# A block of gated cross-attention and FFN on one core: products of the last group reordered by tokens, one sum of M moved

## The chip, the cores and the metric

The kernel runs on one core of a Trainium2 chip. The metric is the device time of one execution in microseconds (us). Engines are named as in the profile: PE is TensorE (PEld its weight loads), DVE is VectorE, ACT is ScalarE, POOL is GpSimd, SP is SyncE, which here only issues transfers.

## The reference, cut to what matters

```python
# x (4, 2048, 512), context (4, 77, 384), 16 heads of 64, all float32
def _layernorm(x): return (x - mean(x)) / sqrt(var(x) + 1e-5)      # over the last axis, 512 wide

def attention(x, context):                    # Wq (512,1024), Wk, Wv (384,1024), Wo (1024,512)
    q, k, v = heads(x @ Wq), heads(context @ Wk), heads(context @ Wv)
    out = softmax(q k^T / 8) v
    return merge(out) @ Wo + bo

def ffn(x):                                   # W (8,512,512), b (8,512): one of eight is picked
    idx = argmax(log_softmax(logits) - log(-log(u)))
    return x @ W[idx] + b[idx]

x = x + tanh(g_xattn) * attention(_layernorm(x), context)
x = x + tanh(g_ffn)   * ffn(_layernorm(x))
```

## The kernel before

The 8192 tokens are worked on in 16 groups of 512; four groups share one context. For each of the four contexts the weights are folded ahead: M stands for Wq with the keys (scores are x times M), vo for the values with Wo. So a group has three large products: the scores (`ps_s`, from the columns of x and M), the attention output (`ps_a`, from the softmax weights `pT` and `vo`), and the FFN (`ps_f`, from the residual stream `xc` and the picked weight `wf`).

Each large product is made by `Seven`, the scheme of seven products of half-size blocks in place of eight. The columns are split in a 2 x 2 grid: B11, B12, B21, B22, where the first digit is the half of the contraction and the second the half of the group's tokens (256 each). T1 to T4 are sums and differences of these (`Columns.sum`: T1 = B12 - B11, T2 = B22 - T1, T3 = B22 - B12, T4 = B21 - T2), made on POOL. On the weights' side blocks 4 to 6 are such sums too, and block 3 becomes one (`weight_sum`: block 5 = 0 - 3, then 3 = 3 + 2, 4 = 3 - 0, 6 = 1 - 4). `ORDER` lists the seven products: block of the weight, column block, PSUM bank r, and whether the bank starts anew:

```python
ORDER = ((0, "B11", 0, True), (3, "T1", 1, True), (4, "T2", 0, False), (1, "B21", 2, True),
         (5, "T3", 0, False), (6, "B22", 1, False), (2, "T4", 0, False))
```

Products that share r accumulate in one bank, and `post` takes intermediate states out: `keep` copies a bank to SBUF on ACT (L469 without, L473 with the bias), or DVE adds a bank to what was kept (L486). The result's quarters are named by two digits: half of the features, half of the tokens.

Around it, in a steady group i, with j = i - 1: the exps of group i run on ACT beside the attention products of group j; DVE transposes between rows and columns (`x_columns` L412, `to_rows` L417, `s_rows` L515, `p_columns` L552); POOL makes the T sums (L437), the scaling of the softmax by its sums (`head_scale` L543) and the residual additions (`residual` L558). `residual_last` (L565) is on DVE, straight from PSUM. `y_rows` turns the residual stream back into rows, `f_rows` the FFN's output. The second layer norm is applied behind the FFN: `Norms` takes statistics of y (`stats` L370), sums them over partitions with two small products on TensorE (`mean`, `var`, L375), and raises to -1/2 on POOL (`rstd` L409). The scaled FFN output (`f_scale` L586, on ACT) is added to y (`f_add` L590) and stored (`store` L594, four transfers for a group, by quarter of the features).

Every engine's queue is in the order in which the code issues (a schedule by hand): an instruction that waits holds all that stands behind it on its engine. In the groups i = 3, 7 and 11 (`swap_m`), M of the next context is loaded (`load_m`) and its four `weight_sum` are made: numbers 0, 2 and 3 on POOL, number 1 on DVE at the end of the attention products (L877).

The last group has no successor whose scores could fill TensorE. Its attention products, its FFN products, and the scaling and storing that remain stand in the tail of the function, from `j, f = NGRP - 1, NGRP - 2` on. There `by_feature` (h = half of the features in a quarter row, v = half of the group's rows) splits the last scaling in four, which are spread over POOL, ACT and DVE by `scaled`. The last transfers are issued as `store(j, 0, 8, ...)` and `store(j, 8, 8, ...)`, each in four transfers of 128 KB over the queues of SP and ACT.

Of the kernel before, what the change touches and what calls it, by code (L numbers as in the profile page):

```python
# [10 lines left out]
AF = mybir.ActivationFunctionType  # L11
ALU = mybir.AluOpType
AX = mybir.AxisListType

P = 128
# [4 lines left out]
def flamingo_block_kernel(  # L20
# [337 lines left out]
    class Norms:  # L358


        def __init__(self, i):
            self.y = 2 <= i
            self.x = i < NGRP
            self.n = NG * (self.y + self.x)
            self.x0 = NG * self.y
            self.s6 = small.tile([P, self.n, 6], F32, tag="s6", name="s6")

# [29 lines left out]
        def rstd(self):  # L397
            self.rs = small.tile([P, self.n], F32, tag="rs", name="rs")
            nc.vector.tensor_scalar(self.rs, self.ps[:, 1], EPS, None, ALU.add)  # L399
            if self.x:  # L400
                r = self.rs[:, ds(self.x0, NG)]
                nc.gpsimd.tensor_tensor(r, r, neghalf, ALU.pow)  # L402
                self.up = small.tile([P, NG], F32, tag="up", name="up")
                self.down = small.tile([P, NG], F32, tag="down", name="down")
                nc.gpsimd.tensor_scalar(self.down, r, -SCALE, None, ALU.mult)
                nc.gpsimd.tensor_scalar(self.up, r, SCALE, None, ALU.mult)
            if self.y:
                r = self.rs[:, :NG]
                nc.gpsimd.tensor_tensor(r, r, neghalf, ALU.pow)  # L409

    def to_columns(dst, src, q):
        nc.vector.transpose(dst[:, q, :].rearrange("p (g c) -> p g c", c=32), src[:, :, ts(q, 32)])  # L412
# [32 lines left out]
    class Seven:  # L445
# [1 line left out]
        ORDER = ((0, "B11", 0, True), (3, "T1", 1, True), (4, "T2", 0, False), (1, "B21", 2, True),  # L447
                 (5, "T3", 0, False), (6, "B22", 1, False), (2, "T4", 0, False))

        def __init__(self, name, w, cols, pairs, snap, bias=None):  # L450
            self.name, self.w, self.cols, self.pairs, self.bias = name, w, cols, pairs, bias
            self.n = len(pairs)
            self.low, self.high = snap
            self.ps = [None] * 3

        def product(self, s):
            blk, cname, r, first = self.ORDER[s]
            if first:
                self.ps[r] = bank(self.name)[:, : self.n * T2].rearrange("p (n t) -> p n t", n=self.n)
            h = self.cols.h  # L460
            for n, pair in enumerate(self.pairs):
                for c in range(h):
                    nc.tensor.matmul(self.ps[r][:, n, :], self.w(blk, c, pair), self.cols(cname, c),  # L463
                                     start=(first and n == 0 and c == 0), stop=(c == h - 1),
                                     skip_group_check=True)
# [11 lines left out]
            return (self.low, self.high)[int(which[0]) - 1][:, :, int(which[1]) - 1, :]  # L477

        def post(self, s):
            if s in (0, 1, 2, 6):  # L480
                which, r = (("11", 0), ("22", 1), ("12", 0), None, None, None, ("21", 0))[s]
                self.keep(self.quarter(which), r, int(which[0]) - 1)
            else:
                which, r = {3: ("11", 2), 4: ("22", 0), 5: ("12", 1)}[s]
                c = self.quarter(which)
                nc.vector.tensor_tensor(c, c, self.ps[r], ALU.add)  # L486

# [276 lines left out]
    for i in range(1, NGRP):  # L764
# [67 lines left out]
        for s in range(7):  # L832
            at.product(s)
            if s == 0:
                pT[j].sum("T2")
                if 0 <= f:
                    f_scale(f, n.rs, 10, 6)
                    f_add(f, 0, NG, nc.gpsimd)
                    store(f)
                head_max(i, 0)  # L840
                head_max(i, 1)
            if s == 1:
                head_max(i, 2)
                head_max(i, 3)
            if 1 <= s:
                e = (0, 10, 20, 32, 44, 56, 64)
                exps(i, e[s - 1], e[s])
            if s == 0 and i == 1:
                weight_sum(vo, 3)
                pT[j].sum("T3")  # L850
            if s == 1 and i == 1:
                scale_wf(wfr)
            if s == 2:
                pT[j].sum("T4")
                if swap_m:
                    weight_sum(m, 0)
                if not last:
                    x_columns(nx)
                    norms[nx].stats(xg[nx], norms[nx].x0, 0, 8)
                head_sum(i, 0)  # L860
                head_scale(i, 0)
            if s == 3:
                if not last:
                    norms[nx].stats(xg[nx], norms[nx].x0, 8, 8)
                    if nx + 1 < NGRP:
                        load(nx + 1)
            if s == 4:
                residual(j, at, "11")
                head_sum(i, 1)
                head_scale(i, 1)  # L870
            if s == 5:
                head_sum(i, 2)
                head_scale(i, 2)
                residual(j, at, "22")
            if s == 6:
                if swap_m:
                    weight_sum(m, 1, nc.vector)  # L877
                residual(j, at, "12")
                residual_last(j, at)
                head_sum(i, 3)  # L880
            else:
                at.post(s)
# [11 lines left out]
        for s in range(6):  # L894
            ff.product(s)
            if s < 2:
                y_rows(j, 2 * s)
            if not last:
                if s == 1:
                    xc[nx].sum("T1")  # L900
                if s == 2:
                    xc[nx].sum("T2")
                if s == 4:
                    if swap_m:
                        weight_sum(m, 2)
                    xc[nx].sum("T3")
                    if swap_m:
                        weight_sum(m, 3)
# [6 lines left out]

    j, f = NGRP - 1, NGRP - 2
    n = norms[NGRP] = Norms(NGRP)
    pT[j].sum("T1")
    at = Seven("ps_a", w_attend, pT[j], (0, 1), SNAP, bo_c)
    for s in range(7):  # L920
        at.product(s)
        if s == 0:
# [13 lines left out]
            pT[j].sum("T4")  # L936
        if s == 3:
            n.rstd()
        if s == 4:
            f_scale(f, n.rs, 0, NG)  # L940
            residual(j, at, "11")
        if s == 5:
            residual(j, at, "22")
            f_add(f, 0, NG, nc.vector)
            store(f)
        if s == 6:
            residual(j, at, "12")
            residual_last(j, at)
            for q in (0, 2):
                y_rows(j, q, 1)  # L950
        elif 0 < s:
            at.post(s)
    yc[j] = Columns(xc[j].all, **{f"T{k + 1}": tq[:, k] for k in range(4)})
    for t in ("T1", "T2", "T3", "T4"):
        yc[j].sum(t)
    n = Norms(NGRP + 1)
    ff = Seven("ps_f", w_ffn, yc[j], (0, 1), SNAP)

    def by_feature(t, h, v):

        return t[:, ts(v, NG // 2), ts(h, D // NA // 2)]

    def scaled(h, v, engine):

        d, y = by_feature(ts_[j], h, v), by_feature(ys[j], h, v)
        r = n.rs[:, ts(v, NG // 2)]
        if engine is nc.vector:
            for g in range(NG // 2):
                nc.vector.scalar_tensor_tensor(y[:, g, :], d[:, g, :], r[:, g : g + 1], y[:, g, :],
                                               ALU.mult, ALU.add)  # L970
            return
        if engine is nc.scalar:
            for g in range(NG // 2):
                nc.scalar.activation(d[:, g, :], d[:, g, :], AF.Copy, scale=r[:, g : g + 1])
            return
        engine.tensor_tensor(d, d, r.unsqueeze(2).to_broadcast(list(d.shape)), ALU.mult)
        engine.tensor_tensor(y, y, d, ALU.add)

    for s in range(6):
        ff.product(s)  # L980
        if s == 0:
            n.stats(ys[j], 0, 8, 8)
            y_rows(j, 0, 0)
            y_rows(j, 2, 0)
            n.stats(ys[j], 0, 0, 8)
            for v in (1, 0):
                y = ys[j][:, ts(v, NG // 2)]
                nc.gpsimd.tensor_tensor(y, y, bf_r.unsqueeze(1).to_broadcast([P, NG // 2, P]), ALU.add)
        if s == 2:
            n.mean()  # L990
            n.spread()
        if s == 3:
            n.var()
            n.rstd()
        ff.post(s)
        if s == 3:
            f_rows(j, ff, 0, 0)
            scaled(0, 0, nc.gpsimd)
        if s == 4:
            f_rows(j, ff, 1, 1)  # L1000
            scaled(1, 1, nc.scalar)
        if s == 5:
            f_rows(j, ff, 0, 1)
            scaled(0, 1, nc.scalar)
    ff.product(6)
    for k in range(2):
        to_rows(ts_[j], ff.ps[0][:, k, :], 2 + k, 0)
    scaled(1, 0, nc.vector)
    store(j, 0, 8, (nc.sync, nc.scalar))
    for h in (1, 0):  # L1010
        y = by_feature(ys[j], h, 1)
        nc.vector.tensor_tensor(y, y, by_feature(ts_[j], h, 1), ALU.add)
    store(j, 8, 8, (nc.sync, nc.scalar))


# [39 lines left out]
```

## Time and profile before

| | |
|---|---|
| runs (us) | 1293.37, 1295.6, 1293.45; median 1293.45 |
| profiled execution | 1293.8 us, of which the span of the instructions is 1291.6 |
| mean granted TensorE clock | 0.993 |
| matmuls: L463 `ps_a`, `ps_s`, `ps_f` | 493.7 us, 294.1 + 222.9 us, 118.8 + 90.8 us |
| bytes moved | HBM read 44.07 MB, written 35.13 MB |
| last attention product's end, last FFN product's end | about 1266.4 and 1281.4 us from the span's start |
| first issue of the last store, last packet moved, end of the span | 1284.06, about 1290.0, 1291.6 |

Lines of a timeline are: start (us from the span's start), duration (us), engine, line of the code, operation, output<-input by the program's names, output shape<-input shapes, count of merged instructions, and in brackets the idle time of the engine just ahead and what ended it. A line of the waits is: who waited <- for whom, total us, times, longest. A line of the table by stretch is: the stretch, its length, then the busy us (and instructions) of PE, PEld, DVE, ACT, POOL, the granted TensorE clock, the busy share of the transfer engines, and GB/s. A matmul in float32 stands in the trace as two instructions, so that one of the seven products is 20 of them in the attention and 8 in the FFN.

### The profile page before, as it was taken

What the parts mean: (1) busy time and instruction counts of PE and PEld (TensorE: products, weight loads), DVE (VectorE), ACT (ScalarE), POOL (GpSimd) and SP (SyncE); (2) the same over time, 40 slices, a digit from 0 to 9 for tenths busy, and PEclk for the clock granted to TensorE, in tenths of its full rate; (3) what the DMA queues carried; (4) which work ended last, traced back from release to release, by engine and by line L of the source; (5) the groups of instructions that cost most, each with busy time, mean ns of one, the idle gap of its engine ahead of it and who ended that gap; (6) DMA issues with size and microseconds to landing.
All of it is one profiled execution on the core that took longest, in us unless ns stands there. A gap on an engine that the chain in (4) does not pass through costs nothing.

```text
span 1291.6 us, 16923 instructions
## 1 busy us (share of the span) xinstructions
PE 1259.6 (98%) x5780; PEld 1072.1 (83%) x5780; DVE 892.2 (69%) x1857; ACT 639.3 (49%) x1741; POOL 875.2 (68%) x481
## 2 busy tenths in 40 slices
PE   9999979999999999999999999999999999999996
PEld 5566758888888888888888888888888888888885
DVE  5669776766767777766767787666767776666555
ACT  3436472644628273553728273553718264463721
POOL 5342478575977688475986787475985787575755
PEclk9999989999999999999999999999999999999999
DMA  9675310112304130022304120032304111010102
GB/s 239 246 256 165 123 33 1 29 38 82 66 1 111 37 65 1 15 52 82 65 1 107 41 55 12 2 64 77 70 1 104 44 40 26 2 33 1 33 1 66
DMA packets 95221, 80.28 MB, mean 62 GB/s; under 512 B 3856, under 2 KB 83088, under 8 KB 95136
## 3 DMA queue, kind: packets, MB, share of 16 engines
q1 hardware_dynamic: 92496, 76.61, 23.1%
q10 hardware_dynamic: 2032, 1.47, 0.4%
q0 software_dynamic: 608, 1.13, 0.4%
q8 instruction: 46, 0.75, 0.2%
q14 instruction: 39, 0.32, 0.1%
HBM read 44.07 MB, written 35.13 MB: 61 GB/s over the span
## 4 chain that ended last, share of the span: by engine, by line
PE 86%; DVE 4%; ACT 4%; DMA 2%; POOL 2%; issue 0%; SPq 0%; DVEq 0%; POOLq 0%; ACTq 0%
PE ps_s L463 36%; PE ps_a L463 32%; PE ps_f L463 14%; ACT s L532 4%; PE ps_vo L336 1%; PE ps_kv L270 1%; PE ps_m L301 1%; POOL xc L558 1%; DMA m<-in_Wk_dram 1%; DVE s L370 1%; DMA xg<-in_x_dram 1%; DVE s L515 1%; DVE sm L539 1%; DVE vo L124 1%; POOL s L543 1%
## 5 line engine op out<-in xcount | busy, mean ns | idle before, releaser
L463 PE MATMUL ps_a<-pT,vo 128*128 128x256 f32 x2240 | 493.7, 383 | 11.4 <-ACT snap L473 5.9
L463 PEld LDWEIGHTS ps_a<-pT,vo 128*128 128x128 f32 x2240 | 428.9, 192 | 72.9 <-POOL wf L124 6.2
L532 ACT ACTIVATE s<-s,nmx,up 128x77 f32<-128x77 f32 x1024 | 355.7, 443 | 6.0 <-DVE nmx L526 6.0
L463 PE MATMUL ps_s<-tq,m 128*128 128x256 f32 x1280 | 294.1, 380 | 0.2 <-DVE m L124 0.2
L437 POOL TENSOR_TENSOR pT<-pT 128x1280 f32<-128x1280 f32 x64 | 187.1, 2924 | 132.1 <-PE ps_a L463 111.2
L463 PEld LDWEIGHTS ps_s<-tq,m 128*128 128x128 f32 x1280 | 241.6, 190 | 35.0 <-issue 2.4
L469 ACT COPY snap<-ps_s 128x512 f32<-128x512 f32 (+1 forms) x188 | 94.5, 512 | 307.9 <-DVE t L417 128.0
L463 PE MATMUL ps_s<-xc,m 128*128 128x256 f32 x960 | 222.9, 381 | 0.6 <-DVE wq L339 0.6
L463 PEld LDWEIGHTS ps_s<-xc,m 128*128 128x128 f32 x960 | 180.8, 190 | 28.9 <-DVE wq L339 2.3
L543 POOL TENSOR_TENSOR s<-s,sm 128x1232 f32<-128x1232 f32 x64 | 145.3, 2271 | 73.8 <-DVE sm L540 64.5
L486 DVE TENSOR_TENSOR snap<-snap,ps_s 128x512 f32<-128x512 f32 (+1 forms) x141 | 83.6, 595 | 85.2 <-PE ps_s L463 83.9
L515 DVE STREAM_TRANSPOSE s<-snap 128x512 f32<-128x512 f32 x156 | 100.0, 686 | 49.3 <-ACT snap L469 47.4
L586 ACT ACTIVATE t<-t,rs 128x128 f32<-128x128 f32 x240 | 73.3, 390 | 98.8 <-POOL rs L409 98.8
L463 PE MATMUL ps_f<-tq,wf 128*128 128x256 f32 x512 | 118.8, 380 | 2.2 <-POOL tq L437 2.2
L552 DVE STREAM_TRANSPOSE pT<-s 128x512 f32<-128x512 f32 x160 | 101.1, 678 | 20.9 <-POOL s L543 20.9
L402 POOL TENSOR_TENSOR rs<-rs,neghalf 128x16 f32<-128x16 f32 x16 | 50.2, 3137 | 94.7 <-DVE rs L399 94.7
L539 DVE TENSOR_REDUCE sm<-s 128x16 f32<-128x1232 f32 x64 | 91.5, 1430 | 29.7 <-ACT s L532 29.7
L463 PEld LDWEIGHTS ps_f<-tq,wf 128*128 128x128 f32 x512 | 96.9, 190 | 16.8 <-POOL tq L437 3.8
L437 POOL TENSOR_TENSOR tq<-xc,tq 128x512 f32<-128x512 f32 x64 | 81.6, 1275 | 39.1 <-PE ps_f L463 32.1
L437 POOL TENSOR_TENSOR tq<-xc 128x512 f32<-128x512 f32 x64 | 81.5, 1274 | 23.8 <-DVE xc L412 17.8
L524 DVE TENSOR_REDUCE ps_st<-s 128x16 f32<-128x1232 f32 x64 | 92.4, 1444 | 2.1
L463 PE MATMUL ps_f<-xc,wf 128*128 128x256 f32 x384 | 90.8, 379 | 0.0
(128 smaller groups left out, 1144.2 us busy)
## 6 DMA issues: line engine op xcount, KB each, us to landing
xg<-in_x_dram SPq DMA_DIRECT2D x64, 256.0 KB, 5.6
out_dram<-y SPq DMA_DIRECT2D x60, 256.0 KB, 4.0
vo<-vo_d SPq DMA_DIRECT2D x16, 640.0 KB, 5.4
m<-m_d SPq DMA_DIRECT2D x12, 640.0 KB, 3.9
vo_d<-vo SPq DMA_DIRECT2D x10, 512.0 KB, 3.5
m_d<-vo SPq DMA_DIRECT2D x4, 960.0 KB, 8.0
vo_d<-wq SPq DMA_DIRECT2D x6, 512.0 KB, 2.8
wq<-in_WqT_dram SPq DMA_DIRECT2D x8, 256.0 KB, 6.0
```

The source lines that it names most:

```text
L402: nc.gpsimd.tensor_tensor(r, r, neghalf, ALU.pow)
L437: (engine or nc.gpsimd).tensor_tensor(self.at[name], self.at[a], self.at[b_], op)
L463: nc.tensor.matmul(self.ps[r][:, n, :], self.w(blk, c, pair), self.cols(cname, c), start=(first and n == 0 and c == 0), stop=(c == h - 1), ...
L469: nc.scalar.copy(dst, self.ps[r])
L486: nc.vector.tensor_tensor(c, c, self.ps[r], ALU.add)
L515: nc.vector.transpose(key_chunk(sc[i], k), cols.rearrange("p (g h r) -> p g h r", h=HA, r=R))
L524: nc.vector.tensor_reduce(mx, head(i, h), AX.X, ALU.max)
L532: nc.scalar.activation(head(i, h)[:, g, :], head(i, h)[:, g, :], AF.Exp, scale=norms[i].up[:, g : g + 1], bias=nmx[h][:, g : g + 1])
L539: nc.vector.tensor_reduce(sm, head(i, h), AX.X, ALU.add)
L543: nc.gpsimd.tensor_tensor(head(i, h), head(i, h), sums[h].unsqueeze(2).to_broadcast([P, NG, J]), ALU.mult)
L552: nc.vector.transpose(pT[i].all[:, k, :].rearrange("p (g h r) -> p g h r", h=HA, r=R), key_chunk(sc[i], k))
L586: nc.scalar.activation(ts_[f][:, g, :], ts_[f][:, g, :], AF.Copy, scale=rs[:, g : g + 1])
```

## The change

There are two parts. In the steady loop, `weight_sum(m, 1, nc.vector)` goes from the end of the attention products (s == 6) to the second step of the FFN products (s == 1), behind the second `y_rows`.

In the last group, both `Seven` take their products in the order `BY_TOKENS`: B11, T1, T2, T3, B22, B21, T4. The quarters 22 and 12 (the second half of the tokens) are then final after the fifth product. The residuals, the rows of y, the statistics (now two `Norms` of half a group, `n1` for the second half, `n0` for the first), the bias, the scaling and the stores follow by halves of the tokens. The second half is stored (three transfers on SP, one on ACT) ahead of the last product; the first half after it (two on SP, two on ACT). The scalings are on ACT but for the last one, on DVE; the additions are all on DVE. `f_scale` of the group before is issued in two parts.

```diff
--- before.py
+++ after.py
@@ -358,10 +358,10 @@
     class Norms:
 
 
-        def __init__(self, i):
+        def __init__(self, i, n=None):
             self.y = 2 <= i
             self.x = i < NGRP
-            self.n = NG * (self.y + self.x)
+            self.n = n or NG * (self.y + self.x)
             self.x0 = NG * self.y
             self.s6 = small.tile([P, self.n, 6], F32, tag="s6", name="s6")
 
@@ -405,8 +405,8 @@
                 nc.gpsimd.tensor_scalar(self.down, r, -SCALE, None, ALU.mult)
                 nc.gpsimd.tensor_scalar(self.up, r, SCALE, None, ALU.mult)
             if self.y:
-                r = self.rs[:, :NG]
-                nc.gpsimd.tensor_tensor(r, r, neghalf, ALU.pow)
+                r = self.rs[:, : min(self.n, NG)]
+                nc.gpsimd.tensor_tensor(r, r, neghalf[:, : min(self.n, NG)], ALU.pow)
 
     def to_columns(dst, src, q):
         nc.vector.transpose(dst[:, q, :].rearrange("p (g c) -> p g c", c=32), src[:, :, ts(q, 32)])
@@ -447,14 +447,17 @@
         ORDER = ((0, "B11", 0, True), (3, "T1", 1, True), (4, "T2", 0, False), (1, "B21", 2, True),
                  (5, "T3", 0, False), (6, "B22", 1, False), (2, "T4", 0, False))
 
-        def __init__(self, name, w, cols, pairs, snap, bias=None):
+        BY_TOKENS = ORDER[:3] + ORDER[4:6] + ORDER[3:4] + ORDER[6:]
+
+        def __init__(self, name, w, cols, pairs, snap, bias=None, order=ORDER):
+            self.order = order
             self.name, self.w, self.cols, self.pairs, self.bias = name, w, cols, pairs, bias
             self.n = len(pairs)
             self.low, self.high = snap
             self.ps = [None] * 3
 
         def product(self, s):
-            blk, cname, r, first = self.ORDER[s]
+            blk, cname, r, first = self.order[s]
             if first:
                 self.ps[r] = bank(self.name)[:, : self.n * T2].rearrange("p (n t) -> p n t", n=self.n)
             h = self.cols.h
@@ -477,11 +480,13 @@
             return (self.low, self.high)[int(which[0]) - 1][:, :, int(which[1]) - 1, :]
 
         def post(self, s):
-            if s in (0, 1, 2, 6):
-                which, r = (("11", 0), ("22", 1), ("12", 0), None, None, None, ("21", 0))[s]
+            blk = self.order[s][0]
+            kept = {0: ("11", 0), 3: ("22", 1), 4: ("12", 0), 2: ("21", 0)}
+            if blk in kept:
+                which, r = kept[blk]
                 self.keep(self.quarter(which), r, int(which[0]) - 1)
             else:
-                which, r = {3: ("11", 2), 4: ("22", 0), 5: ("12", 1)}[s]
+                which, r = {1: ("11", 2), 5: ("22", 0), 6: ("12", 1)}[blk]
                 c = self.quarter(which)
                 nc.vector.tensor_tensor(c, c, self.ps[r], ALU.add)
 
@@ -873,8 +878,6 @@
                 head_scale(i, 2)
                 residual(j, at, "22")
             if s == 6:
-                if swap_m:
-                    weight_sum(m, 1, nc.vector)
                 residual(j, at, "12")
                 residual_last(j, at)
                 head_sum(i, 3)
@@ -895,6 +898,8 @@
             ff.product(s)
             if s < 2:
                 y_rows(j, 2 * s)
+            if s == 1 and swap_m:
+                weight_sum(m, 1, nc.vector)
             if not last:
                 if s == 1:
                     xc[nx].sum("T1")
@@ -915,8 +920,10 @@
 
     j, f = NGRP - 1, NGRP - 2
     n = norms[NGRP] = Norms(NGRP)
+    n1, n0 = Norms(NGRP + 1, NG // 2), Norms(NGRP + 2, NG // 2)
     pT[j].sum("T1")
-    at = Seven("ps_a", w_attend, pT[j], (0, 1), SNAP, bo_c)
+    at = Seven("ps_a", w_attend, pT[j], (0, 1), SNAP, bo_c, Seven.BY_TOKENS)
+    yc[j] = Columns(xc[j].all, **{f"T{k + 1}": tq[:, k] for k in range(4)})
     for s in range(7):
         at.product(s)
         if s == 0:
@@ -936,81 +943,86 @@
             pT[j].sum("T4")
         if s == 3:
             n.rstd()
+            f_scale(f, n.rs, 0, 8)
         if s == 4:
-            f_scale(f, n.rs, 0, NG)
-            residual(j, at, "11")
-        if s == 5:
             residual(j, at, "22")
+            f_scale(f, n.rs, 8, 8)
+        if 0 < s < 6:
+            at.post(s)
+        if s == 4:
             f_add(f, 0, NG, nc.vector)
             store(f)
+        if s == 5:
+            residual(j, at, "12")
+            y_rows(j, 2, 1)
         if s == 6:
-            residual(j, at, "12")
+            residual(j, at, "11")
+            yc[j].sum("T3")
+            y_rows(j, 0, 1)
+            n1.stats(ys[j], -8, 8, 8)
+            y_rows(j, 0, 0)
             residual_last(j, at)
-            for q in (0, 2):
-                y_rows(j, q, 1)
-        elif 0 < s:
-            at.post(s)
-    yc[j] = Columns(xc[j].all, **{f"T{k + 1}": tq[:, k] for k in range(4)})
-    for t in ("T1", "T2", "T3", "T4"):
-        yc[j].sum(t)
-    n = Norms(NGRP + 1)
-    ff = Seven("ps_f", w_ffn, yc[j], (0, 1), SNAP)
+    yc[j].sum("T1")
+    yc[j].sum("T2")
+    ff = Seven("ps_f", w_ffn, yc[j], (0, 1), SNAP, None, Seven.BY_TOKENS)
 
     def by_feature(t, h, v):
 
         return t[:, ts(v, NG // 2), ts(h, D // NA // 2)]
 
-    def scaled(h, v, engine):
-
-        d, y = by_feature(ts_[j], h, v), by_feature(ys[j], h, v)
-        r = n.rs[:, ts(v, NG // 2)]
-        if engine is nc.vector:
-            for g in range(NG // 2):
-                nc.vector.scalar_tensor_tensor(y[:, g, :], d[:, g, :], r[:, g : g + 1], y[:, g, :],
-                                               ALU.mult, ALU.add)
-            return
-        if engine is nc.scalar:
-            for g in range(NG // 2):
-                nc.scalar.activation(d[:, g, :], d[:, g, :], AF.Copy, scale=r[:, g : g + 1])
-            return
-        engine.tensor_tensor(d, d, r.unsqueeze(2).to_broadcast(list(d.shape)), ALU.mult)
-        engine.tensor_tensor(y, y, d, ALU.add)
+    def half_bias(v, engine):
+        y = ys[j][:, ts(v, NG // 2)]
+        engine.tensor_tensor(y, y, bf_r.unsqueeze(1).to_broadcast([P, NG // 2, P]), ALU.add)
+
+    def scaled(h, v, rs):
+        d = by_feature(ts_[j], h, v)
+        for g in range(NG // 2):
+            nc.scalar.activation(d[:, g, :], d[:, g, :], AF.Copy, scale=rs[:, g : g + 1])
+
+    def added(h, v):
+        y = by_feature(ys[j], h, v)
+        nc.vector.tensor_tensor(y, y, by_feature(ts_[j], h, v), ALU.add)
 
     for s in range(6):
         ff.product(s)
         if s == 0:
-            n.stats(ys[j], 0, 8, 8)
-            y_rows(j, 0, 0)
+            n1.mean()
+            n1.spread()
             y_rows(j, 2, 0)
-            n.stats(ys[j], 0, 0, 8)
-            for v in (1, 0):
-                y = ys[j][:, ts(v, NG // 2)]
-                nc.gpsimd.tensor_tensor(y, y, bf_r.unsqueeze(1).to_broadcast([P, NG // 2, P]), ALU.add)
-        if s == 2:
-            n.mean()
-            n.spread()
+            n0.stats(ys[j], 0, 0, 8)
+        if s == 1:
+            n1.var()
+            n1.rstd()
+            yc[j].sum("T4")
+            half_bias(1, nc.vector)
         if s == 3:
-            n.var()
-            n.rstd()
+            n0.mean()
+            n0.spread()
+            half_bias(0, nc.gpsimd)
+        if s == 4:
+            n0.var()
+            n0.rstd()
         ff.post(s)
         if s == 3:
+            f_rows(j, ff, 1, 1)
+            scaled(1, 1, n1.rs)
+        if s == 4:
+            f_rows(j, ff, 0, 1)
+            scaled(0, 1, n1.rs)
+        if s == 5:
+            added(1, 1)
             f_rows(j, ff, 0, 0)
-            scaled(0, 0, nc.gpsimd)
-        if s == 4:
-            f_rows(j, ff, 1, 1)
-            scaled(1, 1, nc.scalar)
-        if s == 5:
-            f_rows(j, ff, 0, 1)
-            scaled(0, 1, nc.scalar)
+            scaled(0, 0, n0.rs)
+            added(0, 1)
+            store(j, 8, 8, (nc.sync, nc.sync, nc.sync, nc.scalar))
     ff.product(6)
     for k in range(2):
         to_rows(ts_[j], ff.ps[0][:, k, :], 2 + k, 0)
-    scaled(1, 0, nc.vector)
+    d = by_feature(ts_[j], 1, 0)
+    nc.vector.tensor_tensor(d, d, n0.rs.unsqueeze(2).to_broadcast(list(d.shape)), ALU.mult)
+    added(0, 0)
+    added(1, 0)
     store(j, 0, 8, (nc.sync, nc.scalar))
-    for h in (1, 0):
-        y = by_feature(ys[j], h, 1)
-        nc.vector.tensor_tensor(y, y, by_feature(ts_[j], h, 1), ALU.add)
-    store(j, 8, 8, (nc.sync, nc.scalar))
 
 
 # ---- launch: one core; inputs and outputs as the reference has them ----
```

## The prediction

> **What bounds the kernel now.** First the busy shares of the page: TensorE is the bound nearly throughout, so a gain must come out of its idle time, or out of the tail behind its last product. Then TensorE's list of waits, in the middle and at the end.
>
> ```profile
> PE 1259.6 (98%) x5780; PEld 1072.1 (83%) x5780; DVE 892.2 (69%) x1857; ACT 639.3 (49%) x1741; POOL 875.2 (68%) x481
> ...
> PE ps_st L375 <- DVE tot L374: 3.8, 4, 2.0
> PE ps_f L463 <- POOL tq L437: 2.2, 3, 0.7
> ```
>
> The second wait occurs three times: in groups i = 3, 7, 11, where M is reloaded. The timeline of the third, then of the next group, which has no sum of M:
>
> ```profile
> 926.01 2.38 DVE L124 TENSOR_TENSOR m<-m 128x1280 f32<-128x1280 f32 x1
> 927.00 3.75 POOL L558 TENSOR_TENSOR xc<-xc,snap 128x512 f32<-128x512 f32 x2
> 929.52 1.89 PE L463 MATMUL ps_f<-xc,wf 128*128 128x256 f32 x8
> 932.15 3.72 PE L463 MATMUL ps_f<-tq,wf 128*128 128x256 f32 x16 [0.74 <-POOL tq L437]
> 935.71 1.89 PE L463 MATMUL ps_f<-xc,wf 128*128 128x256 f32 x8
> 936.95 1.90 DVE L552 STREAM_TRANSPOSE pT<-s 128x512 f32<-128x512 f32 x3 [2.38 <-POOL s L543]
> ...
> 947.38 1.20 ACT L469 COPY snap<-ps_s 128x512 f32<-128x512 f32 x2 [2.25 <-DVE t L417]
> ...
> 1000.98 2.50 POOL L558 TENSOR_TENSOR xc<-xc,snap 128x512 f32<-128x512 f32 x2
> 1003.50 1.89 PE L463 MATMUL ps_f<-xc,wf 128*128 128x256 f32 x8
> ...
> 1008.68 1.89 PE L463 MATMUL ps_f<-xc,wf 128*128 128x256 f32 x8
> ```
>
> See how POOL's two residual additions take 3.75 us beside VectorE's sum of M and 2.50 without it. T1 is late, and the first three FFN products take 935.71 - 929.52 = 6.19 us instead of 5.18. So a swap costs 1.01 us. The starts at i = 3 (343.79 to 349.97) and i = 7 (636.65 to 642.84) give the same: 3.0 us in all. Last, the tail:
>
> ```profile
> 1249.07 17.51 PE L463 MATMUL ps_a<-pT,vo 128*128 128x256 f32 x80
> 1249.13 0.84 ACT L473 ACTIVATE snap<-ps_a,bo_c 128x256 f32<-128x256 f32 x2 [4.97 <-PE ps_a L463]
> ...
> 1268.40 0.59 ACT L469 COPY snap<-ps_f 128x512 f32<-128x512 f32 x1 [8.58 <-POOL tq L437]
> ...
> 1273.80 0.40 PE L375 MATMUL ps_st<-tot,jm 128*128 128x16 f32 x2 [2.03 <-DVE tot L374]
> ...
> 1281.45 0.78 DVE L417 STREAM_TRANSPOSE t<-ps_f 128x256 f32<-128x256 f32 x2 [0.23 <-PE ps_f L463]
> 1282.34 1.65 DVE L969 SCALAR_TENSOR_TENSOR y<-t,rs,y 128x64 f32<-128x64 f32 x8
> 1283.91 1.28 DVE L1012 TENSOR_TENSOR y<-y,t 128x512 f32<-128x512 f32 x2
> ```
>
> After the last product VectorE works to 1285.2 while 1 MB starts to go out at 1284.06. The table by stretch shows the transfer engines full to the end, and the clock behind two gaps of TensorE:
>
> ```profile
> 182.00:186.00 4.00, 3.99 (x10) 3.16 (x11) 1.61 (x7) 4.00 (x13) 4.00 (x2) 0.50 0.01 4
> ...
> 1272.00:1274.00 2.00, 0.20 (x2) 0.21 (x2) 1.71 (x9) 0.44 (x1) 1.35 (x2) 1.00 0.00 0
> 1274.00:1282.00 8.00, 7.42 (x36) 6.24 (x35) 5.90 (x17) 2.32 (x10) 7.17 (x4) 1.00 0.00 1
> ...
> 1288.00:1289.00 1.00, 0.00 (x0) 0.00 (x0) 0.00 (x0) 0.00 (x0) 0.00 (x0) 0.50 1.01 283
> 1289.00:1290.00 1.00, 0.00 (x0) 0.00 (x0) 0.00 (x0) 0.00 (x0) 0.00 (x0) 0.50 0.40 109
> ```
>
> **The change, part A: the sum of M moves.** Write F for the start of the FFN's first product. Now the sum comes after y_rows, at about F+5.05 (in the swap above VectorE's y_rows end there: 934.58 - 929.52). POOL then runs head_scale, F+3.87 to F+6.14 in a group without a sum (1007.37 to 1009.64). In the old place the sum could finish only 1.34 us after POOL's multiply (927.05 to 928.39), so I put it at F+6.14 to F+7.5. POOL's T4 and what follows then start at F+7.5, against F+7.35 before. The further sums of M and the scores' T sums thus keep their old distance from F. VectorE's chain (pT, posts, f_rows) also starts at F+7.5, against F+7.43. TensorE alone comes 1.0 us earlier. Behind that: the scores' copies (947.38 to 948.58, F+17.9 to F+19.06) are released by the end of that VectorE chain and must precede the scores' T3 product, which is then due at F+18.99: a new wait of about 0.15 us. POOL's blk 4 is ready at F+14.2 for a product at F+15.5. A: 3 x (-1.01 + 0.15) = -2.6 us; bounds -3.0 and, if the cover is gone, +1.4 (below).
>
> **Part B: the last group, attention.** In BY_TOKENS, T3 follows T2, and both accumulate in bank r = 0; the old order had B21 in another bank between them. ScalarE must save r = 0 before T3 adds to it. The copies stand at 1249.13 to 1249.97, and T3 would start at 1249.07: a wait of 0.95 us (0.5 if the two halves are released one by one; I take 0.95, as the first copy too began only when the whole product was done). Everything after moves by 0.95. The two halves of f_scale, f_add and its store (SP's issues at 1262.3) keep their places and cost nothing: four attention products lie over them. f_add can now meet POOL's residual 12 and end at 1263.2, just ahead of P5's post at 1263.3; without that cover it costs up to 1. The y_rows of half 2, stats and y_rows of half 1 then fill VectorE up to the last residual, as POOL's 11, T3, T1, T2 (1.27 each) stay ahead of their products. FFN starts at 1267.4.
>
> **Part B: the last FFN**, products 1.73 apart. Two products, to 1270.9, with the first statistics product hidden. Its variance product waits in TensorE's queue for VectorE: spread 0.8, y_rows 0.7, eight stats 1.65, total 0.2, from 1269.5 to 1272.95: idle 2.0, as before at 1273.80. P2 starts 1273.25. Then the same-bank wait again: copy starts 1.98 after the product (1268.40 - 1266.42), takes 0.59: idle 0.9, P3 at 1275.85. P4 at 1277.7. VectorE meanwhile: spread 0.8, post 0.69, f_rows 0.77, total 0.2, to 1280.5; so the second variance product adds a third gap of 1.1, P5 at 1280.8, P6 at 1282.5. From P5's end (1282.8) VectorE is the bound: post 0.69, four additions and one multiply of 0.61 each, f_rows 0.77, to_rows 0.78: 5.3 us, to 1288.1. ScalarE's 8 scalings of 2.0 us each time fit beside it (the last, 1284.9 to 1286.9). The half-size pow on POOL lies between 0.26 (a multiply of that width) and 2.91 (its old size); either ends before its scaling. The half_bias on VectorE, 1.14 (half of 2.28 at L582), lies beside P2. On the queues: SP takes three issues and ScalarE one, at 1285.5 to 1287.4, ScalarE's behind its scaling; both queues are free at 1288.2.
>
> The second store then starts at 1288.2, not 1284.06: +4.1. But only 512 KB remain. Before, the first issue to the last packet took 1284.06 to 1290.0 = 5.9 us for 1 MB; half of the 5 us of moving is saved at the mean rate, more at the 283 GB/s of 1288. I take 3.2 us for it, so -2.7. The Trainium skill (DMA: Bandwidth & Descriptors, Anatomy of one DMA) fits about 2 us plus bytes over 436 GB/s, by which half a MB less saves an estimated 1.2 us, and B would be +2.9. That fit is for GpSimd's queue; the trace has this very transfer and decides. B = 4.1 - 2.7 = +1.4; bounds -0.5 (waits half as long) and +3.
>
> A second rule speaks against B. The trace shows 0.50 of the clock in 182 to 186, after 5.88 us without a product (60 matmuls took 15.78 us there, 13.1 at the 17.51 / 80 of 1249.07), and 1.00 behind the 2.03 us gap. The skill (TensorE: Matmul & The Clock Gate, What's actually happening) halves the clock after about 3.4 us idle. Three gaps of 2.0, 0.9 and 1.1, apart by products, stay under it one by one: 0. Were they counted together, B would be 2.75 dearer.
>
> Sum: -2.6 + 1.4 = -1.2 on the profiled execution (1291.6 span, 1293.8 with what lies around it): 1292.6. The median shown is 0.35 below that one: 1292.3.
>
> **The rivals.** (1) The tail pays: the half-product release, shorter gaps and a store drained at full rate make B about 0; -3.0 gives 1290.4. For: the early half leaves only half the store. Against: VectorE's 5.3 us behind P5. (2) Slower: the sum in its new place loses POOL's interval to T4 as well and VectorE's chain runs 1.34 later; the ScalarE copy then holds the scores' T3 product 1.5 us in each swap, +4.5 - 3.0 + 1.4 = +2.9: 1296.3. It decides once pT starts later than F+8.4. For: that chain has no gap from F+7.43 to F+17.8. Against: at 927.05 VectorE got its turn between two POOL instructions. (3) The clock falls once in the tail: +2.75, 1295.0. (4) POOL's T1 is late for another reason, and A gives 0: 1294.8; against it, groups without the sum have no wait.
>
> **How the numbers follow.** My case 0.57, (1) 0.22, (2) 0.11, (3) 0.05, (4) 0.05. About 0.2% (2.6 us) is what a measurement of this kernel can tell from no change: below 1290.86 lie two thirds of (1) and a sixth of mine, above 1296.04 most of (2) and the upper ends. Faster 0.25, same 0.63, slower 0.12. My case alone spans 1290.8 to 1293.9. Range 1290.0 to 1295.3: it leaves out (2) and the low end of (1).
>
> **What would show it.** Right: no PE wait on POOL tq in three swaps, POOL's residuals at 2.50, FFN's first three products in 5.2 us; a ScalarE copy named as releaser of T3 at some 0.95 and 0.9; three gaps in the last FFN; a first half store near 1285.5, the second near 1288. Wrong: T3 following T2 without a gap, a granted clock under 1.00 before 1282, or new waits of the scores' products on ScalarE over 0.5 us in the swaps.

## The result, and the profile after

| | before | after |
|---|---|---|
| median of 20 runs each (us) | 1293.94 (1292.55 to 1295.6) | 1291.95 (1291.26 to 1294.85) |
| profiled execution: span, time | 1291.6, 1293.8 | 1289.9, 1291.8 |

The ratio after to before is 0.9984, with a 95% interval of 0.9977 to 0.9991: 2.0 us less, a change of under 0.2%. The prediction said 1.2 less (1293.45 to 1292.3). To see where the time went, the two traces are laid side by side at the same instructions (us from the span's start; a swap is a group in which M is reloaded, i = 3, 7 and 11):

| start of | before | after | after less before |
|---|---|---|---|
| first FFN product, i = 3 | 343.79 | 343.40 | -0.39 |
| fourth FFN product, i = 3 | 349.97 | 348.58 | -1.39 |
| fourth FFN product, i = 7 | 642.84 | 640.57 | -2.27 |
| fourth FFN product, i = 11 | 935.71 | 932.56 | -3.15 |
| T2 of the last attention | 1244.53 | 1241.50 | -3.03 |
| first product of the last FFN | 1266.42 | 1264.42 | -2.00 |
| last product | 1279.53 | 1278.99 | -0.54 |
| end of the span | 1291.6 | 1289.9 | -1.7 |

The first row is no part of the change: over the runs below, that start varies between 343.1 and 345.2. From there to the last attention's T2 lies part A: -3.03 + 0.39 = -2.64. From T2 to the end lies part B: 48.4 instead of 47.07, +1.33. The prediction had -2.6 and +1.4.

The busy line of the page, then TensorE's list of waits. The three waits on POOL's tq in the swaps are gone. The one still listed is another, at 199.09 in the first group: the trace of before has none there, that of part A alone (below) one of 0.17, and it lies ahead of the first row of the table. Two waits on ScalarE's snap, one in each product of the last group, are new; of the 8.5 us of the first line, 7.6 are one wait at 181.64 that the kernel before has too (5.88 at 182.01).

```profile
PE 1256.4 (97%) x5784; PEld 1069.5 (83%) x5784; DVE 893.6 (69%) x1860; ACT 640.6 (50%) x1749; POOL 873.3 (68%) x479
...
PE ps_a L466 <- ACT snap L476: 8.5, 2, 7.6
...
PE ps_st L375 <- DVE tot L374: 3.5, 5, 1.4
...
PE ps_f L466 <- POOL tq L437: 1.1, 1, 1.1
PE ps_f L466 <- ACT snap L472: 0.7, 1, 0.7
```

The timeline of the third swap, after the change:

```profile
924.85 2.50 POOL L563 TENSOR_TENSOR xc<-xc,snap 128x512 f32<-128x512 f32 x2
927.38 1.89 PE L466 MATMUL ps_f<-xc,wf 128*128 128x256 f32 x8
929.10 3.62 PE L466 MATMUL ps_f<-tq,wf 128*128 128x256 f32 x16
...
932.35 2.52 DVE L124 TENSOR_TENSOR m<-m 128x1280 f32<-128x1280 f32 x1
932.56 1.89 PE L466 MATMUL ps_f<-xc,wf 128*128 128x256 f32 x8
...
933.47 2.52 POOL L437 TENSOR_TENSOR tq<-xc,tq 128x512 f32<-128x512 f32 x1
...
934.79 1.89 DVE L557 STREAM_TRANSPOSE pT<-s 128x512 f32<-128x512 f32 x3
...
945.20 1.07 ACT L472 COPY snap<-ps_s 128x512 f32<-128x512 f32 x2 [2.48 <-DVE t L417]
...
946.42 1.96 PE L466 MATMUL ps_s<-tq,m 128*128 128x256 f32 x8
...
948.23 4.48 PE L466 MATMUL ps_s<-xc,m 128*128 128x256 f32 x20
```

POOL's residuals are back at 2.50 and the FFN's first three products at 932.56 - 927.38 = 5.18. VectorE's sum is listed from 932.35 with 2.52, but its end, 934.87, is 1.35 behind the end of POOL's multiply (933.52); POOL's T4 then needs 2.52 for an addition of 1.27, so now T4 bears the wait, and it has time. The last three lines are what is paid: ScalarE's copies end at 946.27, 0.15 ahead of the scores' T3 product, and that product takes 948.23 - 946.42 = 1.81 to the next instead of 1.73.

The tail after:

```profile
1246.10 0.84 ACT L476 ACTIVATE snap<-ps_a,bo_c 128x256 f32<-128x256 f32 x2 [4.97 <-PE ps_a L466]
...
1247.08 17.51 PE L466 MATMUL ps_a<-pT,vo 128*128 128x256 f32 x80 [0.89 <-ACT snap L476]
...
1256.82 2.29 DVE L595 TENSOR_TENSOR y<-y,t 128x2048 f32<-128x2048 f32 x1
1256.83 3.41 POOL L563 TENSOR_TENSOR xc<-xc,snap 128x512 f32<-128x512 f32 x1 [3.05 <-DVE snap L491]
...
1269.64 0.39 PE L375 MATMUL ps_st<-tot,jm 128*128 128x8 f32 x2 [1.38 <-DVE tot L374]
...
1270.31 2.56 POOL L409 TENSOR_TENSOR rs<-rs,neghalf 128x8 f32<-128x8 f32 x1 [4.15 <-DVE rs L399]
...
1272.59 1.99 PE L466 MATMUL ps_f<-tq,wf 128*128 128x256 f32 x8 [0.73 <-ACT snap L472]
...
1276.94 0.39 PE L375 MATMUL ps_st<-tot,jm 128*128 128x8 f32 x2 [0.40 <-DVE tot L374]
...
1279.19 0.69 DVE L491 TENSOR_TENSOR snap<-snap,ps_f 128x512 f32<-128x512 f32 x1 [0.26 <-PE ps_f L466]
...
1283.31 1.29 DVE L984 TENSOR_TENSOR y<-y,t 128x512 f32<-128x512 f32 x2
1284.63 0.89 ACTq L599 DMA_DIRECT2D out_dram<-y  x2
```

T3 waits for ScalarE's copy twice (1247.08, 1272.59), and TensorE waits twice for VectorE's totals (1269.64, 1276.94). From 1279.19 VectorE works without a break up to the second store at 1284.63. The table by stretch shows that store's transfers:

```profile
1283.00:1284.00 1.00, 0.00 (x0) 0.00 (x0) 0.91 (x3) 0.27 (x2) 0.00 (x0) 0.82 1.07 277
...
1287.00:1288.00 1.00, 0.00 (x0) 0.00 (x0) 0.00 (x0) 0.00 (x0) 0.00 (x0) 0.50 0.96 252
1288.00:1288.50 0.50, 0.00 (x0) 0.00 (x0) 0.00 (x0) 0.00 (x0) 0.00 (x0) 0.50 0.17 45
```

The early half moves at 1283, while VectorE still computes, and the last packets are through at about 1288.3, 3.67 us after the second store's first issue.

### The profile page after: what moved, and what is told of

It reads as the page before. It is cut to its first block, busy times and chain, and to the rows that moved or that the text cites. A ratio compares the mean times of both kernels' runs of the same rounds, so it can differ in the third digit from the quotient of the medians.

```text
span 1289.9 us, 16937 instructions
## 1 busy us (share of the span) xinstructions
PE 1256.4 (97%) x5784; PEld 1069.5 (83%) x5784; DVE 893.6 (69%) x1860; ACT 640.6 (50%) x1749; POOL 873.3 (68%) x479
## 3 DMA queue, kind: packets, MB, share of 16 engines
q0 software_dynamic: 608, 1.13, 0.4%
q10 hardware_dynamic: 1760, 1.34, 0.3%
## 4 chain that ended last, share of the span: by engine, by line
PE 89%; DVE 4%; ACT 3%; DMA 2%; SPq 0%; POOL 0%; issue 0%; DVEq 0%; ACTq 0%; POOLq 0%
PE ps_s L466 36%; PE ps_a L466 35%; PE ps_f L466 15%; ACT s L537 2%; PE ps_vo L336 1%; PE ps_kv L270 1%; PE ps_m L301 1%; DMA xg<-in_x_dram 1%; DVE s L370 1%; DMA wq<-in_WqT_dram 1%; DVE s L520 1%; DVE vo L124 1%; PE ps_st L375 0%; DVE pT L557 0%; DMA m<-in_Wk_dram 0%
## 5 line engine op out<-in xcount | busy, mean ns | idle before, releaser
L437 POOL TENSOR_TENSOR tq<-xc,tq 128x512 f32<-128x512 f32 x64 | 85.2, 1332 | 39.3 <-PE ps_f L466 32.2
```

The source lines that it names most:

```text
L437: (engine or nc.gpsimd).tensor_tensor(self.at[name], self.at[a], self.at[b_], op)
```

## The experiments

In what follows a tail is measured within its own trace, from T2 of the last attention to the end of the span, so that the start of the kernel plays no part. T2 starts, before and after:

```profile
1244.53 4.56 PE L463 MATMUL ps_a<-pT,vo 128*128 128x256 f32 x20
...
1241.50 4.56 PE L466 MATMUL ps_a<-pT,vo 128*128 128x256 f32 x20
```

The tail is 47.07 us before and 48.40 after. Each is one execution; the two kernels below that have the tail of before with its longest gap filled by products that nothing reads have 46.75 and 46.89, so differences of 0.3 are not read.

### One part at a time

Part A alone is the kernel before with

```diff
-                if swap_m:
-                    weight_sum(m, 1, nc.vector)
...
+            if s == 1 and swap_m:
+                weight_sum(m, 1, nc.vector)
```

> The kernel before with only VectorE's sum of M moved into the FFN products (part A alone). My theory: each of three swaps loses its 1.0 us wait of TensorE on POOL's T1 and gives back some 0.13 us at the scores' T3 and B22 products, where ScalarE's copies come late: -2.6 us against before (ratio 0.998), FFN's first product to its fourth 5.2 us in i = 3, 7, 11. Rival (the tail is what gained, the sum's wait only moves): within 0.5 us of before.

Measured: ratio 0.9978 (0.9969 to 0.9986), 2.8 us less. The FFN's fourth product is at 348.45 and 932.44, and T2 at 1241.39: the starts of the changed kernel within 0.13 us.

Part B alone is the changed kernel with these lines put back.

> The changed kernel with the sum of M back in its old place (part B alone). My theory: slower than before by 1.3 us (ratio 1.001): TensorE waits 0.9 and 0.7 us for ScalarE's copy between T2 and T3, the last store starts about 3.6 us later than before and drains in 2.2 us less. Rival (the tail gained): faster than before by 1.7 us or so.

Measured: ratio 0.9998 (0.9987 to 1.0008). So the tail did not gain, but +1.3 us (1.0010) is just outside the interval, too. In the trace the tail is 1293.0 - 1244.62 = 48.4, +1.3 as expected; what differs is the runs of before, and that is taken up below with the clock. The two parts together make the change: -2.6 and +1.3 in the span.

### What the sum costs in its new place

```diff
-            if s == 1 and swap_m:
-                weight_sum(m, 1, nc.vector)
```

> The changed kernel without VectorE's sum of M (block 3 is not replaced by 3 + 2, so the scores of the later contexts are not the reference's). One look at the trace: my theory is that each swap gains the same 1.0 us of the FFN's start, and that the 0.1 us now lost between the scores' B21, T3 and B22 products (946.42 to 948.23 is 1.81 where 1.73 is usual) goes, 0.3 to 0.4 us in all. Rival: these gaps have another cause and stay.

TensorE's timeline in the third swap of this kernel:

```profile
946.23 1.89 PE L466 MATMUL ps_s<-xc,m 128*128 128x256 f32 x8
947.95 1.89 PE L466 MATMUL ps_s<-tq,m 128*128 128x256 f32 x8
949.68 1.67 PE L466 MATMUL ps_s<-xc,m 128*128 128x256 f32 x7
```

The starts are 1.72 and 1.73 apart, where the changed kernel has 1.78 (944.64 to 946.42) and 1.81. From the fourth FFN product of i = 3 to T2 of the last attention it takes 1242.95 - 350.41 = 892.54, the changed kernel 892.92 and part A alone 892.94: 0.38 for three swaps, in one profiled execution without the sum. There ScalarE's copy ends 0.93 us ahead of the T3 product (947.02), not 0.15, which fits the copies as the cause.

### The order within the tail

```diff
-        BY_TOKENS = ORDER[:3] + ORDER[4:6] + ORDER[3:4] + ORDER[6:]
+        BY_TOKENS = ORDER[:3] + ORDER[5:6] + ORDER[4:5] + ORDER[3:4] + ORDER[6:]
...
-            residual(j, at, "22")
+            residual(j, at, "12")
...
-            f_rows(j, ff, 1, 1)
-            scaled(1, 1, n1.rs)
+            f_rows(j, ff, 0, 1)
+            scaled(0, 1, n1.rs)
```

B22 now comes ahead of T3, so quarter 12 is final before quarter 22; in the left-out lines too, the two change places in the residuals, y_rows, f_rows, scaled and added.

> The changed kernel with B22 taken ahead of T3 in the last group (B11, T1, T2, B22, T3, B21, T4; the work on quarters 12 and 22 exchanged to match), so that no product follows another in the bank that ScalarE has still to copy. My theory: both waits of TensorE on ScalarE's copies (0.89 and 0.73 us) are gone and the end comes 1.2 to 1.6 us earlier than in the changed kernel, 3.0 to 3.5 us under before (ratio 0.9975). Rival (VectorE alone sets the tail's end, the bank waits lie beside it): the waits go, the end stays within 0.4 us of the changed kernel.

TensorE's timeline, first T2's end in the attention, then T2, B22 and T3 of the FFN:

```profile
1246.27 0.29 PE L375 MATMUL ps_st<-tot,jm 128*128 128x16 f32 x2
1246.41 5.86 PE L466 MATMUL ps_a<-pT,vo 128*128 128x256 f32 x26
...
1269.23 1.97 PE L466 MATMUL ps_f<-tq,wf 128*128 128x256 f32 x8
1271.04 1.89 PE L466 MATMUL ps_f<-xc,wf 128*128 128x256 f32 x8
1272.77 0.28 PE L375 MATMUL ps_st<-tot,jm 128*128 128x8 f32 x2
1272.90 1.97 PE L466 MATMUL ps_f<-tq,wf 128*128 128x256 f32 x8
```

Both waits are gone, and the rival with them: the tail is 1288.2 - 1241.87 = 46.33, 2.07 less (ratio to before 0.9966, 0.9952 to 0.9979). That is more than I expected, since I had added the idle times of the list (0.89 + 0.73). These count from the modelled end of a pipelined product. From start to start, T2 to the next product was 5.58 and is 4.54 in the attention, was 2.71 and is 1.81 in the FFN: 1.04 + 0.90 = 1.94.

The other edit moves the variance's sum in VectorE's queue:

```diff
             n1.spread()
-            y_rows(j, 2, 0)
-            n0.stats(ys[j], 0, 0, 8)
         if s == 1:
             n1.var()
+            y_rows(j, 2, 0)
             n1.rstd()
+            n0.stats(ys[j], 0, 0, 8)
```

> The changed kernel with VectorE's sum for the second half's variance (and its small product) issued ahead of the first half's rows and statistics. My theory: TensorE's gap of 1.4 us ahead of the last FFN's T2 product goes; the first half's statistics then come later on VectorE, but have room until its mean product; the end comes 0.8 to 1.4 us earlier than in the changed kernel. Rival (VectorE alone sets the tail's end): within 0.4 us of the changed kernel.

Ratio to before 0.997 (0.9958 to 0.9982). T1 to T2 in the FFN takes 1.95 (1266.85 to 1268.80) instead of 3.59, and the tail is 1288.8 - 1242.06 = 46.74, 1.66 less: again the whole distance from start to start, not the 1.38 of the list. The statistics found room elsewhere on VectorE.

Then both edits together:

> The changed kernel with both repairs: B22 ahead of T3, and the variance's sum ahead of the first half's rows and statistics. My theory (TensorE's gaps of 0.89, 0.73 and 1.38 us lie on the path, so the two add up): span 2.6 to 2.9 us under the changed kernel, 1287.0 to 1287.3 where that has 1289.9, about 4.5 us under before. Rival (once the same-bank waits are gone VectorE is the bound and the second repair is worth nothing more): within 0.5 us of B22 ahead of T3 alone, 1288.2.

TensorE's timeline of the kernel with both edits:

```profile
1265.25 1.97 PE L466 MATMUL ps_f<-tq,wf 128*128 128x256 f32 x8
1267.06 0.28 PE L375 MATMUL ps_st<-tot,jm 128*128 128x8 f32 x2
1267.20 1.97 PE L466 MATMUL ps_f<-tq,wf 128*128 128x256 f32 x8
1269.01 1.89 PE L466 MATMUL ps_f<-xc,wf 128*128 128x256 f32 x8
...
1273.26 0.39 PE L375 MATMUL ps_st<-tot,jm 128*128 128x8 f32 x2 [0.41 <-DVE tot L374]
```

The tail is 1286.2 - 1241.49 = 44.71, 3.69 less than the changed kernel's, and 2.07 + 1.66 = 3.73: the gaps add up. So TensorE's gaps are on the path, and VectorE bounds the tail only from the sixth FFN product on. The ratio to before is 0.9951 (0.9937 to 0.9964), median 1288.45: this version beats both kernels.

### The early store

```diff
-            store(j, 8, 8, (nc.sync, nc.sync, nc.sync, nc.scalar))
...
     store(j, 0, 8, (nc.sync, nc.scalar))
+    store(j, 8, 8, (nc.sync, nc.scalar))
```

> The changed kernel, but its early store of the second half is issued behind the first half's at the very end. My theory: 1 MB then drains from 1284.6 on as in the kernel before (5.9 us from first issue to last packet, against 3.7 in the changed kernel): 2.2 us slower than the changed kernel, span 1292.1. Rival (transfers of that size hide in the fixed cost of the last one): at most 0.7 us slower.

The stores then also go evenly over the two queues, as before. The ratio to before is 0.9995 (0.9986 to 1.0003). The tail is 1291.6 - 1241.18 = 50.42, 2.0 longer than the changed kernel's. The table by stretch has 1 MB to move again:

```profile
1286.00:1288.00 2.00, 0.00 (x0) 0.00 (x0) 0.00 (x0) 0.00 (x0) 0.00 (x0) 0.50 0.92 216
1288.00:1290.00 2.00, 0.00 (x0) 0.00 (x0) 0.00 (x0) 0.00 (x0) 0.00 (x0) 0.50 0.86 236
```

So the early half is what pays for the later start of the last store: without it part B would cost 3.3 us.

### The granted clock in the tail

Most spans of before, and those of part A alone, fall in two groups, and the groups differ in the mean granted clock. The profiled execution of part A alone suggests a reason. Its gap ahead of the mean product is the old one, 2.03 us, at 1268.6 to 1270.66. TensorE's timeline, then the table by stretch, with the clock as the third column from the end:

```profile
1270.66 0.40 PE L375 MATMUL ps_st<-tot,jm 128*128 128x16 f32 x2 [2.03 <-DVE tot L374]
1270.90 2.94 PE L463 MATMUL ps_f<-xc,wf 128*128 128x256 f32 x8
1273.64 0.45 PE L375 MATMUL ps_st<-tot,jm 128*128 128x16 f32 x2
```

```profile
1268.00:1270.00 2.00, 0.62 (x3) 0.19 (x2) 1.97 (x10) 0.59 (x1) 1.80 (x1) 1.00 0.00 0
1270.00:1272.00 2.00, 1.34 (x7) 1.18 (x8) 1.38 (x8) 0.00 (x0) 1.55 (x1) 0.94 0.00 0
1272.00:1274.00 2.00, 2.00 (x8) 1.65 (x6) 0.09 (x1) 0.00 (x0) 0.80 (x1) 0.50 0.00 0
1274.00:1276.00 2.00, 2.00 (x8) 1.72 (x8) 1.54 (x4) 0.00 (x0) 1.62 (x1) 0.71 0.00 0
```

The two products behind the gap take 2.74 and 2.42, from start to start, instead of 1.81 each: its tail is 48.71, not 47.07, 1.64 longer. Three kernels test this. The first two fill the gap with products that nothing reads; part A alone is the base of the first, the kernel before that of the second:

```diff
         if s == 2:
+            ps = bank("ps_w")
+            for _ in range(4):
+                nc.tensor.matmul(ps[:, :T2], w_ffn(0, 0, 0), yc[j]("B11", 0), start=True, stop=True)
             n.mean()
```

> Only the sum moved (the old tail), and four more products of 128x128 by 256 that nothing reads, put in TensorE's gap of 2.03 us ahead of the last group's mean product, about 1.7 us of work. Theory: in some half of the executions the gap lets the granted clock fall to 0.50 for some 3.4 us (as in the profiled run with the sum alone), which makes two groups of spans 1.9 us apart; filled, the gap is gone, all spans lie near the fast group, 1287.9 to 1288.7, mean clock 0.992 or more. Rival (the two groups come from the start of the kernel or from transfers): two groups of spans as before, 1288.3 and 1290.2.

> The kernel before, with the same four unread products in its gap of 2.03 us ahead of the last mean product, and nothing else. Theory (the gap lets the clock fall in about half of the executions): spans in one group, 1290.7 to 1291.9, mean clock 0.993, and a median some 1 us under that of before, whose own runs fall again in two groups, about 1291.1 and 1293.0. Rival (the two groups have another cause): two groups here too.

The third lengthens the gap of the changed kernel:

```diff
             n0.stats(ys[j], 0, 0, 8)
+            n0.stats(ys[j], 0, 0, 8)
```

> The changed kernel with the first half's statistics taken twice (eight more instructions of VectorE, 1.65 us, same result), which stand ahead of the variance's sum: TensorE's gap there goes from 1.38 to 3.0 us. Theory: the gap is on the path, +1.6 us, and a gap of that length lets the granted clock fall to 0.50 in half of the executions or more, for 1.5 to 2 us more: spans in two groups, about 1291.6 and 1293.4, the latter with a mean clock of 0.990 to 0.991. Rival (the clock has nothing to do with this gap): one group at 1291.6.

Runs whose mean clock is 0.991 or less, over all the runs (one run of before, of 4717 us, is left out). The mean is over the whole span and holds the kernel's start too, where the same 60 products take 15.78 us in the trace of before and 14.62 in that of after; so the table counts low means, and that they stand for falls in the tail is a reading:

| tail | kernels | longest gap in the last FFN | runs at 0.991 or less |
|---|---|---|---|
| old | before (three times), part A alone | 2.03 us | 34 of 78 |
| old, gap filled | the two with fillers | under 0.5 us | 3 of 18 |
| new | after, part B alone, B22 first, variance early, both, late store | 1.38 us or less | 2 of 62 |
| new, gap lengthened | statistics twice | 2.93 us | 7 of 13 |

The profiled execution with the longer gap, at 1268.9 to 1271.84:

```profile
1270.00:1272.00 2.00, 0.16 (x1) 0.16 (x1) 1.79 (x10) 0.00 (x0) 0.00 (x0) 0.80 0.00 0
1272.00:1278.00 6.00, 5.27 (x13) 3.83 (x14) 1.38 (x3) 0.58 (x1) 5.28 (x3) 0.50 0.01 3
1278.00:1282.00 4.00, 4.00 (x13) 3.29 (x13) 1.10 (x5) 0.00 (x0) 0.81 (x1) 0.57 0.00 0
```

The fillers on part A alone left one group in five runs, 1287.8 to 1288.9, close to what was expected (ratio to before 0.9966, 0.9952 to 0.9979). On the kernel before (0.9994, 0.9985 to 1.0003) three of 13 runs stayed at 1293.4 to 1293.8 with 0.991: that expectation failed in part, and what lowered the clock in these three no trace shows. The longer gap did worse than expected: 1291.5 to 1297.6 (1.0007, 0.9996 to 1.0019), and in its profile the clock stays low for some 10 us, through the gaps that follow. So a longer gap brings more low clocks: the third kernel differs from the changed one in this gap alone, and has 7 of 13 where the new tails have 2 of 62. That filling the old gap takes them away is less sure: 0 of 5 against 7 of 12 on part A alone, but 3 of 13 against 9 of 25 for before run beside it, which chance can give. That the gap is the only cause is not shown.

This accounts for the run of part B alone. Among runs at 0.992 or more, the median span in that comparison is 1291.2 for before and 1292.4 for part B alone: the +1.3 of the trace. Half of the runs of before have the lower clock and are about 2 us longer, and that hid it. (The runs are chosen here by their clock; the trace is the firmer ground.)

## Why the prediction was right

**Part A.** Predicted 3 x (-1.01 + 0.15) = -2.6; measured -3.02 + 0.38 = -2.64. The slot of the sum behind POOL's multiply, the late T4, the unchanged VectorE chain, and the wait of the scores' products on ScalarE's copies came as written, the last as 0.05 and 0.08 us at two products instead of 0.15 at one. Rival (2), the chain 1.34 later, did not occur: pT starts at F+7.41 (934.79 - 927.38). Rival (4) is out by the waits.

**Part B.** Predicted +1.4, measured +1.33. The path is the one described, with TensorE's gaps, VectorE behind the last products and a half store; that the sum comes out so close is luck, for two errors of half a microsecond cancel, the last store's later start and its drain:

| step | predicted | measured |
|---|---|---|
| T3's wait in the attention | 0.95 | 1.04 |
| FFN: T1 to T2 | 4.0 | 3.59 |
| FFN: T2 to T3 | 2.6 | 2.71 |
| FFN: fifth to sixth product | 3.1 | 2.62 |
| VectorE's post of the sixth product to the second store | 5.4 | 5.44 |
| T2 of the attention to second store | 43.7 | 43.13 |
| second store's first issue to last packet | 3.2 | 3.67 |
| last packet to end of span | 1.6 | 1.6 |

The totals over half a group take VectorE 0.12 to 0.17 each and overlap with what follows, where I had taken the spread at 0.8 and the total at 0.2 from rows of full width. The step on the drain was too hopeful: 512 KB take 3.67 against 5.94 for 1 MB, 2.27 saved, not 2.7. The fit that the Trainium skill gives (DMA: Bandwidth & Descriptors, Anatomy of one DMA), by which I had estimated 1.2 saved, was further off; the trace's row was the better guide. f_add met POOL's residual as warned, the other way round: VectorE went first at 1256.82 and POOL's addition took 3.41 instead of 1.27. It ended at 1260.24, just ahead of the next post at 1260.31, and so cost nothing. The pow of half width is 1.65 where nothing is beside it, a little over half of 2.91; the other, 2.56 at 1270.31, starts beside VectorE's half_bias, which ends at 1271.37. Rival (1), a tail worth about 0, is not refuted by the times of part B alone (ratio 0.9998); the traces refute it, with 48.40 and 48.38 against 47.07.

**What the sum did not contain.** It gave -1.2, the medians -2.0. The median span of runs at 0.992 or more is 1290.05 for the changed kernel and 1291.15, 1291.5 and 1291.5 for before in the three comparisons: it moved by 1.1 to 1.5, and the summed -1.2 lies within that. Two things come on top. The time around the span (the run's time less its span) is 2.2 us for before and the three kernels with its tail, and 1.9 for the changed kernel and all others with the new tail: -0.3. I took it as fixed; its cause was not tried (it is not the store's split over the queues, as the late store has 1.9 as well). And the clock: I weighed the rule of the Trainium skill (TensorE: Matmul & The Clock Gate, What's actually happening: a fall after about 3.4 us idle) for the three new gaps, took 0, and that held for them. But I did not ask it of the kernel before, whose own gap of 2.03 us goes with a lower clock in many executions, though not in the one that I had. The rule's figure does not hold here: the measurement decides, and a gap of 2.03 us was at times followed by a fall. So rival (3) had its sign reversed, and its size too large: 1.64 us in the trace of part A alone, not 2.75 (and 15.78 - 13.1, from which the 2.75 came, is 2.7). With the change the low clocks are all but gone; they went with about 2 us in some four of ten runs of before.

## What to carry to other kernels

When products are reordered, look at which of them share an accumulator: two in a row, with a copy to be taken between them, put the copy's whole time on the path, and one product from another bank between them takes it off again. Count a gap of TensorE from start to start, and ask for the first instruction in another engine's queue that it waits for; here one total stood behind ten instructions that nobody needed yet. And when one profile of the kernel before shows a full clock, look at the clocks of its other runs too before costing its gaps at nothing.

## What the runs showed that I had not expected

A gap of 2.03 us in TensorE's products was followed by a granted clock of 0.50 for about 3.4 us in one profiled execution (part A alone) and by 1.00 in another (before); by the mean clocks it is low in 34 of 78 runs. Where the longest gap in the last FFN is 1.38 us or less, it is low in 2 of 62, with one of 2.93 us in at least 7 of 13.

That VectorE's addition of two SBUF operands and a POOL instruction beside it hold each other up was in the prediction; that either can be the one that waits was not. VectorE's sum of M, which takes 1.48 us at its shortest, is listed with 2.52 and ends 1.35 behind POOL's multiply; POOL's addition of 1.27 is listed with 3.41 and ends 1.13 behind VectorE's, which took 2.29. So the listed time holds the wait.
